# A scan's layernorm: its shift taken from VectorE's written order to GpSimd, behind the power

## The chip, the core and the metric

The kernel runs on one core of a Trainium2 chip. The metric is device time in microseconds (us), the median of several executions. The core has five engines that each work through a queue of their own: TensorE (PE, with its weight loads shown as PEld), VectorE (DVE), ScalarE (ACT), GpSimd (POOL) and SyncE (SP), which here only issues DMA transfers.

## The reference

There are 32 sequences of 256 tokens and 256 channels. A scan block comes first, two layers of windowed attention with a gated feed-forward part follow, and the input is added at the end. Cut to what matters:

```python
def scan_block(x, t_emb, ...):
    xr, gate = split(x @ W_in.T, 2)                  # 512 channels each
    xc = silu(conv4(xr + t_emb[:, None, :]))         # along the tokens
    mu, var = xc.mean(-1), xc.var(-1)
    xn = (xc - mu) / sqrt(var + 1e-5) * ln_g + ln_b  # the norm of this case
    Bm, Cm, dt = split(xn @ W_xproj.T, 3)            # 16 states each
    Ad = 1 + 0.01 * tanh(dt @ W_dt.T + b_dt) * A
    Bd = Bm * minimum(norm(xn), 1)
    # for every token: h = clip(h*Ad + Bd*xn, -10, 10); y = Cm . h
    return (y + D * xn) * silu(gate) @ W_out.T

def layer(x):                                        # twice
    q, k, v = split(shift_token(x) @ wqkv, 3)        # 8 heads of 64
    q, k = rotary(l2norm(q) * qs, l2norm(k) * ks)
    x = x + local_attention(q, k, v) @ wo            # window 128
    a, g = split(layernorm(shift_token(x)) @ w1 + b1, 2)
    return x + (a * gelu(g)) @ w2 + b2

out = x + layer(layer(scan_block(x, cond)))
```

## The kernel before

**Tiling.** The sequences form 4 groups of 8. A group's scan runs over 256 tokens in 8 chunks of 32 steps, so there are 32 chunks and 1024 steps in all. A step (`step`, L716) is one VectorE instruction of a custom form that updates the state h of 8 sequences by 16 states (128 partitions) over 512 channels. Its input comes from a scratch tensor `xnd` in DRAM, which holds the normed tokens of the chunk: `load_rows` (a DMA, `xrep<-xnd`) spreads one token's rows over the states, and ScalarE scales the tile (L706). TensorE reads the outcome out (`y`, L728).

**The norm of the scan.** A chunk has 256 token rows (8 sequences by 32 tokens), normed as two tiles of 128 rows, j = 0 and 1, which makes 64 norms. Each is a chain over four engines and a store:

1. `norm_turn`: TensorE transposes xc into `tp_x` (L548).
2. `norm_stats`: VectorE takes mean and variance into `mv` (bn_stats L558, bn_aggr L560) and adds the epsilon (`ve`, L562); GpSimd raises this to the power -1/2 (L565) into the first column of `stat`, the scale.
3. `norm_shift`: VectorE multiplies -mean by that scale (L571) into the second column of `stat`, the shift.
4. `norm_apply`: ScalarE computes xn = scale * tp_x + shift (L579).
5. `norm_affine`: GpSimd multiplies by ln_g and adds ln_b (L586, L587).
6. `norm_out`: SP stores xn to `xnd` (L591), and ScalarE sums the squares (L593).

**Attention and feed-forward.** While a group's scan runs, the sequences of the group before pass through the two layers, two sequence-layers for each chunk; so the first group's scan (`alone`) runs by itself, and after the last scan step only layers remain. Names that come up later: `ps_qkv` (L989) is the projection; `rotated` squares q or k (`sq`, L1002, ScalarE), forms `rot` and `swp` (L1005, L1010, VectorE) and finishes them on GpSimd (L1013, power `rn` L1021, L1022); `sc` and `pT` are scores and their exponentials (L1205, L1214; GpSimd masks them at L1225); `rs`, `ov` sum and multiply with the values (L1239, L1258); `divide` (L1282, VectorE) multiplies the heads' outputs `oT` by `rb`, the inverses of the sums; `ps_wo` (L1039) is the output projection; `pa` (L1362) is the feed-forward's first product, `ag` its GELU on ScalarE (L1373, with a load of the function's table) and then the gated product on VectorE (L1380); `po_f` (L1389) is the second product. In the second layer `fo` is that outcome (L1400, VectorE), GpSimd adds the input to it (L1408) and SP stores it (L1409). `sq`, `swp` and `fo` rotate through one set of three buffers, with the tag "swp". Of the scan, `xd` loads the normed rows for the skip term (L745), which GpSimd scales (L758), and `ps_in` (L399), the convolution's `acc` (L478, L489), `tz`, `zT` (L785, L799) and `ps_out` (L808) are its input and output parts.

**What sets the order.** The work of the scan is entered in slots, one for each step, by `at(s, what, ...)`; that of the layers in stages, by `stage(...)`. With s0 a chunk's first step, the norm j of that chunk has s = s0 - 26 + 4j; statistics stand in slot s+2, the shift in s+4, the application in s+5, the affine passes in s+6 and the store in s+9. The program is recorded in this order, and a list scheduler then chooses each engine's order by what it expects to be ready. `tc.keep_in_program_order(...)` takes an instruction out of this choice: it is held behind the instruction that was recorded before it on its engine. The shift L571 is held so, which puts it behind the scan step of slot s+4 on VectorE, and so are the scalings L706, the masks, `divide` and a few others. Every engine then works through its instructions in the order thus fixed.

Of the kernel before, what the change touches and what calls it, by code (L numbers as in the profile page):

```python
# [14 lines left out]
ALU = mybir.AluOpType  # L15
# [58 lines left out]
def kernel(  # L74
# [29 lines left out]
    nc = tc.nc  # L104
# [117 lines left out]
    def program(ctx, exact):  # L222
# [154 lines left out]
        def group_scan(g):  # L377
# [12 lines left out]
            ck = [{} for _ in range(NCH)]  # L390

            def at(s, what, *args):
                agendas[-1].setdefault(s, []).append(partial(what, *args))
# [161 lines left out]
            def norm_stats(c, j):  # L555
                tp, stat = ck[c]["tp", j], ck[c]["stat"]
                st = sm.tile([P, 6], FP, tag="st", name="st")
                nc.vector.bn_stats(st, tp)  # L558
                mv = sm.tile([P, 2], FP, tag="mv", name="mv")
                nc.vector.bn_aggr(mv, st)  # L560
                ve = sm.tile([P, 1], FP, tag="ve", name="ve")
                nc.vector.tensor_scalar_add(  # L562
                    ve, mv[:, 1:2], LN_EPS if alone else 4 * LN_EPS
                )
                nc.gpsimd.tensor_tensor(stat[:, j, 0:1], ve, neg_half[:, 0:1], ALU.pow)  # L565
                ck[c]["mv", j] = mv

            def norm_shift(c, j):
                stat, mv = ck[c]["stat"], ck[c].pop(("mv", j))
                tc.keep_in_program_order(  # L570
                    nc.vector.scalar_tensor_tensor(  # L571
                        stat[:, j, 1:2], mv[:, 0:1], -1.0, stat[:, j, 0:1], ALU.mult, ALU.mult
                    )
                )

            def norm_apply(c, j):
# [279 lines left out]
            for c in range(NCH):  # L856
                s0 = c * CH
                for hb in range(CH // TB):
                    s = s0 + hb * TB
                    for i in range(NI):  # L860
                        at(s + 4 * i + 5, read_out, c, hb, i)
                    at(s + 21, gated, c, hb)
                    at(s + 25, out_gate, c, hb)
                    at(s + 11, skip, c, hb)
                for ch in range(NC_):
                    at(s0 - 38 + 2 * ch, conv_in, c, ch)
                    at(s0 - 37 + 2 * ch, conv_taps, c, ch)
                    at(s0 - 36 + 2 * ch, conv_th, c, ch)
                    if not alone:
                        at(s0 - 35 + 2 * ch, conv_out, c, ch)  # L870
                for ch, s in enumerate((13, 16, 17, 18)):
                    at(s0 + s + 2, gate_th, c, ch)
                    if not alone:
                        at(s0 + s + 4, gate_out, c, ch)
                at(s0 - 25, raw_copy, c)
                at(s0 - 24, raw_turn, c)
                for j in range(NJ):
                    s = s0 - 26 + 4 * j
                    at(s + 2, norm_stats, c, j)
                    at(s + 4, norm_shift, c, j)  # L880
                    at(s + 5, norm_apply, c, j)
                    at(s + 6, norm_affine, c, j)
                    at(s + 9, norm_out, c, j)
                at(s0 - 11, length, c)
                at(s0 - 9, figures, c)
                at(s0 - 7, figures_in, c)
                at(s0 - 6, decay_th, c)
                at(s0 - 5, decays, c)
                at(s0 - 4, put_c, c, 0)
                at(s0 + 4, put_c, c, 1)  # L890
                for d in range(KM):
                    at(s0 + 45 + 2 * d, copy_y, c, d)
                    at(s0 + 46 + 2 * d, put_y, c, d)
            agendas.append({})
            for c in range(NCH):
# [20 lines left out]
                for hb in range(CH // TB):  # L916
                    s = s0 + hb * TB
# [5 lines left out]
            if alone:  # L923
                n = (NG - 1) * NCH * 2
                for u in range(n):
                    s = -30 + u * (NCH * CH) // n
# [6 lines left out]
        def scan_slots(groups):  # L933


            slots, scans = {}, [group_scan(g) for g in groups]
            for part in range(2):
                for i, agendas in enumerate(scans):
                    for s, what in agendas[part].items():
                        slots.setdefault(i * S + s, []).extend(what)  # L940
            for s in range(min(slots), max(slots) + 1):
                for what in slots.get(s, ()):
                    what()
                yield s
# [705 lines left out]
```

## Time and profile before

| | |
|---|---|
| median of 3 runs | 3600.9 us (3593.78 to 3604.1) |
| profiled execution | 3604.19 us, its span 3602.5 us |
| mean granted TensorE clock | 0.989 |
| TensorE from 0 to 310, 310 to 600 us | 274.7 of 310, 257.7 of 290 us busy |
| TensorE from 600 to 2810, 2810 to 3602 us | 2146.2 of 2210, 784.6 of 792 us busy |
| VectorE from 600 to 2810 us | 1781.0 of 2210 us busy |
| power L565 | 64 times, 541 to 1124 ns, median 562 |
| shift L571 | 64 times, 145 to 1264 ns, median 153 |
| application L579 | 64 times, 745 to 778 ns, median 777 |

The profile is of one execution, so times taken from it are set against its 3604.19 us. The span runs from the first to the last instruction, and 1.7 us of the execution lie around it. In a view of a line the three durations are the least, the median and the largest in ns; below them stands how long the engine sat idle before the line's instructions, with the releaser, the total and the number of times; and who waited for them. In a timeline a line gives start and duration in us, engine, line, operation, and "out<-in" with partitions by elements; the bracket tells idle time before it and what ended it. In the chain a line is start, length and what ran. "x8" means eight instructions in a row merged.

### The profile page before, as it was taken

The page shows a single profiled execution, that of the slowest core. Times are in us where ns is not written, and L with a number is a line of the kernel's source. Part 1 is how long each engine was busy: PE and PEld are TensorE (multiplying, and loading weights), DVE is VectorE, ACT ScalarE, POOL GpSimd, SP SyncE. Part 2 cuts the span into 40 slices and gives each one's busy share as a digit, 9 for nine tenths or more (in the row PEclk, how much of TensorE's full clock was granted, in tenths as well). Part 3 has the DMA queues.
Part 4 walks back from the last instruction along what each step waited for, and adds up shares of the span by engine and source line. Part 5 has one row for each costly group of instructions (what it writes and reads, how often), then busy time and mean ns, then how long its engine had stood idle before and what let it go on. Part 6 is the DMA issues. An engine that isn't in the chain of part 4 may idle for free.

```text
span 3602.5 us, 57609 instructions
## 1 busy us (share of the span) xinstructions
PE 3463.1 (96%) x20220; PEld 2254.4 (63%) x20220; DVE 2667.7 (74%) x5049; ACT 2148.9 (60%) x3659; POOL 1884.7 (52%) x1842
## 2 busy tenths in 40 slices
PE   7999988999999999999999999999999999999999
PEld 4545335666666666666666666666666677777777
DVE  5888889878888777887787888877877545555553
ACT  4656656666666666666666666666666544444543
POOL 4433466545556555655565556555544444443451
PEclk9999999999999999999999999999999999999999
DMA  7788755444454545444454555544454212011111
GB/s 201 210 217 219 200 154 148 133 110 138 131 140 130 149 140 146 130 114 126 117 140 128 135 149 137 142 106 130 116 141 123 61 38 61 13 30 39 31 27 37
DMA packets 468766, 435.67 MB, mean 121 GB/s; under 512 B 228723, under 2 KB 308084, under 8 KB 468340
## 3 DMA queue, kind: packets, MB, share of 16 engines
q1 hardware_dynamic: 384018, 419.88, 42.4%
q10 hardware_dynamic: 84450, 12.01, 2.0%
q8 instruction: 163, 2.67, 0.3%
q14 instruction: 135, 1.11, 0.1%
HBM read 383.54 MB, written 46.66 MB: 119 GB/s over the span
## 4 chain that ended last, share of the span: by engine, by line
PE 59%; DVE 19%; POOL 7%; DMA 7%; ACT 5%; issue 3%; SPq 0%; ACTq 0%; DVEq 0%; POOLq 0%
PE ps_qkv L989 12%; PE pa L1362 12%; DVE h L716 7%; PE po_f L1389 7%; DMA xrep<-xnd 5%; PE ps_wo L1039 4%; PE y L728 4%; PE ov L1258 3%; PE sc L1205 3%; DVE acc L489 3%; PE ps_out L808 2%; ACT xrep L706 2%; PE tr_qk L1028 2%; PE ps_in L399 2%; POOL rn L1021 2%
## 5 line engine op out<-in xcount | busy, mean ns | idle before, releaser
L716 DVE CUSTOM_DVE_ANT_0 h<-h,xrep,lim 128x512 f32<-128x512 f32 x1024 | 959.2, 937 | 219.2 <-ACT xrep L706 185.1
L706 ACT ACTIVATE xrep<-xrep,beta 128x512 f32<-128x512 f32 x960 | 674.2, 719 | 366.6 <-DMA xrep<-xnd 281.3
L989 PE MATMUL ps_qkv<-qkv,res 128*128 128x512 f32 x1536 | 718.5, 603 | 25.2 <-DVE ag L1380 9.8
L1362 PE MATMUL pa<-hT,w 128*128 128x256 f32 (+1 forms) x2816 | 679.9, 383 | 0.0
L1362 PEld LDWEIGHTS pa<-hT,w 128*128 128x128 f32 (+1 forms) x2816 | 516.2, 189 | 147.0 <-issue 53.8
L1013 POOL TENSOR_TENSOR rot<-rot,swp 128x512 f32<-128x512 f32 x256 | 340.1, 1328 | 442.7 <-DVE swp L1010 297.8
L989 PEld LDWEIGHTS ps_qkv<-qkv,res 128*128 128x128 f32 x1536 | 281.2, 191 | 314.1 <-issue 239.4
L1021 POOL TENSOR_TENSOR rn<-ss,neg_half 128x8 f32<-128x8 f32 x256 | 459.0, 1793 | 17.0 <-DVE ss L1019 6.9
L728 PE MATMUL y<-h,ly 128*32 128x512 f32 x2048 | 347.0, 611 | 18.9 <-DVE h L716 17.5
L1314 POOL TENSOR_TENSOR rstd<-ve,neg_half 128x2 f32<-128x2 f32 x64 | 47.0, 734 | 605.1 <-DVE ve L1312 587.7
L1389 PE MATMUL po_f<-ag,w 128*128 128x256 f32 x1280 | 309.7, 389 | 5.5 <-DVE fo L1400 4.3
L1022 POOL TENSOR_TENSOR rot<-rot,rn 128x512 f32<-128x512 f32 x256 | 289.3, 1130 | 19.9
L1380 DVE SCALAR_TENSOR_TENSOR ag<-pa,b_sb,ag 128x256 f32<-128x256 f32 x320 | 152.2, 476 | 195.8 <-ACT ag L1373 195.8
L1389 PEld LDWEIGHTS po_f<-ag,w 128*128 128x128 f32 x1280 | 237.3, 192 | 70.8 <-DVE xc L509 11.7
L1002 ACT ACTIVATE sq<-ps_qkv 128x512 f32<-128x512 f32 x256 | 151.9, 595 | 208.1 <-PE ps_qkv L989 145.5
L1373 ACT ACTIVATE ag<-pa,b_sb 128x256 f32<-128x256 f32 x320 | 150.1, 469 | 179.5 <-PE pa L1362 177.4
L489 DVE SCALAR_TENSOR_TENSOR acc<-xr,wc_sb,acc 128x256 f32<-128x256 f32 x384 | 197.7, 543 | 68.2 <-POOL acc L478 67.6
L1039 PE MATMUL ps_wo<-oT,wo 128*128 128x256 f32 x1024 | 231.6, 379 | 0.0
L1005 DVE TENSOR_TENSOR rot<-ps_qkv,rc_sb 128x512 f32<-128x512 f32 x256 | 174.5, 681 | 68.1 <-ACT sq L1002 67.9
L1214 ACT ACTIVATE pT<-sc 128x512 f32<-128x512 f32 x384 | 208.4, 596 | 6.8 <-PE sc L1205 4.8
L1039 PEld LDWEIGHTS ps_wo<-oT,wo 128*128 128x128 f32 x1024 | 194.6, 190 | 27.1 <-PE y L728 0.8
L1205 PEld LDWEIGHTS sc<-qT,kT 64*64 64x64 f32 (+1 forms) x2816 | 134.8, 159 | 114.6 <-issue 89.2
(159 smaller groups left out, 5689.8 us busy)
## 6 DMA issues: line engine op xcount, KB each, us to landing
xrep<-xnd SPq DMA_DIRECT2D x960, 256.0 KB
rb<-inv SPq DMA_DIRECT2D x128, 256.0 KB
xnd<-xn SPq DMA_DIRECT2D x64, 256.0 KB
qkv<-in_wqkv_dram SPq DMA_DIRECT2D x24, 512.0 KB
ahead<-xs_a SPq DMA_DIRECT2D x48, 256.0 KB
xp<-ahead SPq DMA_DIRECT2D x48, 256.0 KB
xd<-xnd SPq DMA_DIRECT2D x192, 64.0 KB
w<-in_w_dram SPq DMA_DIRECT2D x80, 128.0 KB
```

Of the source, the lines that this page charges most:

```text
L489: nc.vector.scalar_tensor_tensor(acc, xr[:, :, k : k + CH], wc_sb[:, ch, k : k + 1], acc, ALU.mult, ALU.add,)
L706: scaled = nc.scalar.activation(bx, ck[c].pop(("bx", t), bx), AF.Copy, scale=ck[c]["beta"][:, t : t + 1])
L716: nc.vector._custom_dve(TENSOR_ADD_SAT, out=h_new, in0=state["h"], in1=bx, s0=ck[c]["lim"][:, 0, t : t + 1], s1=ck[c]["lim"][:, 1, t : t + 1],
L728: nc.tensor.matmul(ck[c]["y", hb][32 * q : 32 * q + 32, :], ly[hb % 2][:, 32 * t : 32 * t + 32], ck[c].pop(("h", hb * TB + t)), start=(i = ...
L989: nc.tensor.matmul(ps, res[b][:, k, t0 : t0 + W], wt["qkv", a][:, k], start=(k == 0), stop=(k == KM - 1),)
L1013: nc.gpsimd.tensor_add(rot, rot, swp)
L1021: nc.gpsimd.tensor_tensor(rn, ss, neg_half, ALU.pow)
L1022: nc.gpsimd.tensor_mul(rot, rot, bc(rn, 2, DH))
L1039: nc.tensor.matmul(po[:, d], wt["wo", 0][:, c, d * P : (d + 1) * P], oT[:, c, :], start=(c == 0), stop=(c == NC_ - 1),)
L1205: nc.tensor.matmul(banks[r][k0 : k0 + mk, i, q0:q1], kT[rows, i0 + i, kw * W + k0 : kw * W + k0 + mk], qT[rows, i0 + i, kw * W + q0 : kw * ...
L1362: nc.tensor.matmul(dst[x], wt["w1", m][:, k, x], self.h[:, k], start=(k == 0), stop=(k == KM - 1),)
L1389: nc.tensor.matmul(self.po[:, d], wt["w2", 0][:, m, d * P : (d + 1) * P], self.ag[m], start=(m == 0), stop=(m == len(MCH) - 1),)
```

## The change

The shift is computed by GpSimd, as a tensor_scalar with two multiplications (mean times scale times -1), recorded directly behind the power. The slot entry for it, its function and its hold in VectorE's order are gone, and the mean no longer has to be handed on through `ck`.

```diff
@@ norm_stats
                 nc.gpsimd.tensor_tensor(stat[:, j, 0:1], ve, neg_half[:, 0:1], ALU.pow)
-                ck[c]["mv", j] = mv
-
-            def norm_shift(c, j):
-                stat, mv = ck[c]["stat"], ck[c].pop(("mv", j))
-                tc.keep_in_program_order(
-                    nc.vector.scalar_tensor_tensor(
-                        stat[:, j, 1:2], mv[:, 0:1], -1.0, stat[:, j, 0:1], ALU.mult, ALU.mult
-                    )
+                nc.gpsimd.tensor_scalar(
+                    stat[:, j, 1:2], mv[:, 0:1], stat[:, j, 0:1], -1.0, ALU.mult, ALU.mult
                 )
@@ the slots of a chunk
                 for j in range(NJ):
                     s = s0 - 26 + 4 * j
                     at(s + 2, norm_stats, c, j)
-                    at(s + 4, norm_shift, c, j)
                     at(s + 5, norm_apply, c, j)
                     at(s + 6, norm_affine, c, j)
                     at(s + 9, norm_out, c, j)
```

## The prediction

> **What bounds the kernel now.** The page first. Its first part lists each engine's busy time, its fourth the chain of work that ended last, by engine:
>
> ```profile
> PE 3463.1 (96%) x20220; PEld 2254.4 (63%) x20220; DVE 2667.7 (74%) x5049; ACT 2148.9 (60%) x3659; POOL 1884.7 (52%) x1842
> ...
> PE 59%; DVE 19%; POOL 7%; DMA 7%; ACT 5%; issue 3%; SPq 0%; ACTq 0%; DVEq 0%; POOLq 0%
> ```
>
> TensorE is 96% busy, yet holds only 59% of the chain, so stages differ. From 2810 us on there is no scan, and nothing of the change. While scan and attention run side by side a chunk lasts about 103 us (one sequence's ps_wo stands at 1624.13, the next chunk's at 1726.55, the next at 1829.61). One such chunk in the chain, start and length:
>
> ```profile
> 1716.40 3.43 PE ps_qkv L989 x8
> ...
> 1732.60 1.73 PE pa L1362 x8
> ...
> 1748.79 1.73 PE ps_qkv L989 x4
> 1750.54 0.60 ACT sq L1002
> 1751.17 0.69 DVE rot L1005
> ```
>
> From 1700 to 1750 every link is TensorE, back to back; from 1750 to 1801 the chain runs through ACT, DVE, POOL and the xrep transfer, and starts from TensorE's last product. So in the first half a delay elsewhere is free while it is shorter than TensorE's slack, and what exceeds it shifts the second half one to one. The changed instruction stands in the first half. Its own line view:
>
> ```profile
> L571 DVE SCALAR_TENSOR_TENSOR stat<-mv,stat x64: 145/153/1264, 30.2 to 2657.8; 128x1 f32<-128x1 f32 x64
> ...
>   POOL stat L565: 41.9, 22
> ...
>   ACT xn L579: 105.9, 38
> ```
>
> DVE sat idle 41.9 us for POOL's power in 22 of 64 cases, and ACT 105.9 us for the shift in 38. These are the apparent prize. Neither is on the chain above.
>
> **What the skill says.** (1) "SBUF — State Buffer", section "Who interferes with whom": DVE and GpSimd have one port pair that is locked for a whole instruction; a DVE instruction with two SBUF inputs holds off a GpSimd one that reads SBUF. The trace agrees: the power L565 takes 541 ns at best and 1124 at most, fo L1408 1259 to 2226. (2) "TensorE: Matmul & The Clock Gate", "Architectural detail": ACT, DVE and GpSimd take their queues strictly in order. The timelines below agree: ACT stands still with later work ready.
>
> **The change, part by part.** *Removed:* 64 DVE instructions of 153 ns (18.9 us busy, many overlapped with a neighbour) and the 41.9 us of waits. *Added:* 64 POOL instructions. The trace has no such form on one column; the nearest row is lim L660, a tensor_scalar on 32 columns:
>
> ```profile
> L660 POOL TENSOR_SCALAR lim<-pi x32: 291/296/617, 45.1 to 2708.0; 128x32 f32<-128x32 f32 x32
> ```
>
> I take 0.29 us; at most 0.62 as there, at least 0.1 (POOL's 128x2 memset takes 0.09). 64 x 0.29 = 19 us on an engine that is 52% busy. By itself I cost it at nothing, under POOL's idle time; without that cover it is 0.3 us per norm, the 19 us. The hop from POOL back to DVE goes; POOL follows itself after 0.08 us, as L587 does L586.
>
> *Moved,* as the order that the scheduler gives each engine in the two kernels shows (settled when a kernel is built; there is no time in it). On DVE and TensorE nothing else moves from chunk 10 on. On POOL the shift, and xn's two affine passes L586/L587, come directly behind the power, ahead of fo L1408 where that stood between. On SP the store of xn follows them ahead of fo's store L1409. On ACT, for the first norm (j=0) of chunks 18 to 31, **xn L579 moves ahead of the GELU's table load, ag L1373 and sq L1002**, with two xrep scalings behind it. Before, ACT did those during the power; in the new order it waits. ACT, layer 0, before:
>
> ```profile
> 1714.77 1.28 ACT L1373 ACT_TABLE_LOAD   x1
> 1716.43 0.47 ACT L1373 ACTIVATE ag<-pa,b_sb 128x256 f32<-128x256 f32 x1 [0.38 <-PE pa L1362]
> 1718.15 0.60 ACT L1002 ACTIVATE sq<-ps_qkv 128x512 f32<-128x512 f32 x1 [1.24 <-PE ps_qkv L989]
> 1718.64 0.77 ACT L579 ACTIVATE xn<-tp_x,stat 128x512 f32<-128x512 f32 x1
> ```
>
> DVE and POOL there:
>
> ```profile
> 1717.15 1.22 DVE L1282 TENSOR_TENSOR oT<-oT,rb 128x1024 f32<-128x1024 f32 x1
> 1718.29 0.15 DVE L571 SCALAR_TENSOR_TENSOR stat<-mv,stat 128x1 f32<-128x1 f32 x1
> 1718.36 0.48 DVE L1380 SCALAR_TENSOR_TENSOR ag<-pa,b_sb,ag 128x256 f32<-128x256 f32 x1
> ```
>
> ```profile
> 1716.20 1.05 POOL L565 TENSOR_TENSOR stat<-ve,neg_half 128x1 f32<-128x1 f32 x1 [0.90 <-DVE ve L562]
> ```
>
> *Layer 0 (8 chunks: 20 to 23, 28 to 31).* The power ends at 1717.25, just after L1282 (two SBUF inputs) has begun; the POOL shift is held off to 1718.37 and ends at 1718.65, 0.2 later than DVE's. ACT, free at 1714.75, waits 3.9 us; then xn to 1719.4, two xreps to 1720.65, table load to 1721.95, ag to 1722.44: 5.5 us later than before (1716.90). The product L1380 starts at 1722.5, +4.1. All DVE work behind it (rot, swp, ss) is 3.8 to 4.2 late, and hence POOL's rn and rot, the power of j=1 (queued behind them) and its xn, +2.8. TensorE's slack, time from each input's end to the matmul that takes it: tp_x after L1380 5.3, pa after the first swp 4.5, ps_wo after the second 3.6 against 3.8 late, **ov after the second xn 1.74 against 2.8**. So +1.1 us a chunk (0.2 to 2). DVE's vanished wait for j=1 (2.67 us) is spent on this lateness.
>
> *Layer 1, which writes the output (6 chunks: 18, 19, 24 to 27).* POOL and ACT before:
>
> ```profile
> 2233.60 1.04 POOL L565 TENSOR_TENSOR stat<-ve,neg_half 128x1 f32<-128x1 f32 x1 [0.91 <-DVE ve L562]
> 2234.71 2.18 POOL L1408 TENSOR_TENSOR fo<-fo,xs 128x512 f32<-128x512 f32 x1
> ```
>
> ```profile
> 2236.94 0.78 ACT L579 ACTIVATE xn<-tp_x,stat 128x512 f32<-128x512 f32 x1 [0.74 <-DVE stat L571]
> ...
> 2240.42 0.60 ACT L1002 ACTIVATE sq<-ps_qkv 128x512 f32<-128x512 f32 x1 [2.09 <-POOL xn L587]
> ```
>
> The releaser named is doubtful: sq and fo share a rotating buffer ("swp", three deep), and the second sq may only start when fo is stored, 3.5 us after fo's end at 2236.89. The view of fo's tile has the same:
>
> ```profile
>   ACT sq L1002: 39.3, 24
> ```
>
> In the new order the shift ends at about 2236.05 (0.9 earlier than now), xn runs to 2236.8, its affine passes to 2239.6, and only then fo to 2240.9: 4.0 later. Its store lands at 2244.4, and the second sq and swp are 4.0 late. ps_wo has 1.31 us of slack there: **+2.7 us a chunk** (0 to 3.7: nothing if the store isn't what frees the buffer). SP's queue stops at fo's store 4 us longer; behind it stand weight loads, xd's four loads (issued from 2238.80, wanted by POOL's L758 only at 2249.10, so 0 while they are less than about 5 us late) and xrep loads, which are not issued before 2246.47 as it is: 0. The other TensorE inputs late there (3.0 to 3.6 of slack against about the same lateness, ov 0.8) fit within those 2.7.
>
> *Chunks 8 to 17:* many places differ, xn mostly earlier and fo later. I take -2 (-10 to +10), a choice. *First 600 us, scan alone:* the shift stood 2.3 and 4.7 us behind its power in DVE's order without a stall; 20 of them cost DVE 0.15 us each, and xn comes up to 3 us sooner, but is not on the chain (xrep transfer 17.4%, scan step 16.9% of it). I take -3 (-6 to 0). *After 2810 us:* 0.
>
> Sum: 6 x 2.7 + 8 x 1.1 - 2 - 3 = 16.2 + 8.8 - 5 = +20. The profiled execution took 3604.2 us (span 3602.5, 1.7 around it), 3.3 above the median of the three runs, 3600.9 (3593.8 to 3604.1). Against itself the sum is 3624; against the median, which I forecast, **3621**. About 0.3%, 11 us, is what a measurement of this kernel can tell from no change.
>
> **Rivals.**
> (a) *Faster:* the j=1 stall is the real limiter. TensorE waits for DVE's ag, h and ag again (sc 19.4, y 17.5, ps_qkv 9.8, ov 7.5: 54 us in its list of waits). If half of DVE's 41.9 us is behind those, and ACT's new wait hides, the result is 3601 - 21 = 3580, with a third 3587. For it: POOL's power for j=1 and its DVE wait hold the scan steps behind them. Against: DVE then meets a 2.83 us wait for xrep at 1736.58, so that the time is only passed on. It decides if ACT's ag comes less than about 1.3 us late, not 5.5.
> (b) *Nothing:* slacks are wider than read (the releaser at 2240.42 is right after all, and xn j=1 makes good its delay): +0 to +9, about 3603.
> (c) *Much slower:* the shift is held off by a scan step or L1282 in every chunk, ACT stops each time, and chunks 8 to 17 lose as the later ones do: 24 x 2 = 48, 3649.
> That the shift is not moved at all is excluded: the order has it behind each power.
>
> **How the numbers follow.** The likeliest case (+11 to +33) gets 0.45, (c) 0.10, (b) 0.20, (a) 0.25. Slower by over 0.3%: 0.55; within: 0.20; faster: 0.25. Own range of the likeliest: 3612 to 3634. The range to hold 8 in 10 leaves out the far ends of (a) and (c): 3581 to 3646.
>
> **What would show it.** Right: in the profile after, no L571 on DVE; POOL's shift about 0.3 us, over 1 us where L1282 runs; ACT's idle time before xn grows above the 111.7 us it has before from all causes, ag's product late; fo's store later and ps_wo of layer 1 about 2.7 late within its chunk; TensorE busy time unchanged, chunks 24 to 27 longest in growth. Wrong: chunks of 103 us or less in 2200 to 2600 us, or xn without a wait on ACT; then (b) or (a).

## The result, and the profile after

The changed kernel takes 3634.1 us in the median of six runs (3630.5 to 3641.3), against 3600.9 us before (3593.8 to 3608.7). The ratio is **1.0095, with a 95% interval of 1.0082 to 1.0108**: 33 us slower. The profiled execution has a span of 3636.1 us, and its scan ends 33.9 us later than before's; what follows the last scan step takes the same 791 us in both.

First the parts of the page that were shown of before, busy times and the chain by engine:

```profile
PE 3474.4 (96%) x20220; PEld 2258.5 (62%) x20220; DVE 2653.5 (73%) x4985; ACT 2147.0 (59%) x3659; POOL 1912.4 (53%) x1906
...
PE 51%; DVE 18%; POOL 13%; DMA 7%; ACT 6%; issue 4%; SPq 0%; ACTq 0%; DVEq 0%; POOLq 0%
```

No engine has got appreciably more work: DVE lost 14 us, POOL gained 28. But TensorE's share of the chain has gone from 59 to 51%, and POOL's from 7 to 13%. The chain now leaves TensorE in a part of the chunk where it used not to.

In the changed file the lines from the norm's application on stand 6 or 7 lower: the shift is L566 (POOL), xn L573, ag L1366 (ACT) and L1373 (DVE), `divide` L1275, sq L995, ps_wo L1032, ov L1251, fo's addition L1401. The line view of the new shift:

```profile
L566 POOL TENSOR_SCALAR stat<-mv,stat x64: 259/444/1146, 32.3 to 2693.3; 128x1 f32<-128x1 f32 x64
...
  ACT xn L573: 182.3, 50
```

DVE's 41.9 us of waits for the power are gone from its list. **ACT's wait for the shift has grown from 105.9 us (38 times) to 182.3 us (50 times).** A chunk with layer 0, the same place as before, first ACT:

```profile
1734.60 0.72 ACT L700 ACTIVATE xrep<-xrep,beta 128x512 f32<-128x512 f32 x1 [1.53 <-issue]
1739.09 0.78 ACT L573 ACTIVATE xn<-tp_x,stat 128x512 f32<-128x512 f32 x1 [3.76 <-POOL stat L566]
1739.76 1.32 ACT L700 ACTIVATE xrep<-xrep,beta 128x512 f32<-128x512 f32 x2
1741.10 1.28 ACT L1366 ACT_TABLE_LOAD   x1
1742.40 0.47 ACT L1366 ACTIVATE ag<-pa,b_sb 128x256 f32<-128x256 f32 x1
```

DVE and then POOL in the same stretch:

```profile
1737.71 1.21 DVE L1275 TENSOR_TENSOR oT<-oT,rb 128x1024 f32<-128x1024 f32 x1
1742.90 0.48 DVE L1373 SCALAR_TENSOR_TENSOR ag<-pa,b_sb,ag 128x256 f32<-128x256 f32 x1 [3.98 <-ACT ag L1366]
```

```profile
1736.76 1.04 POOL L565 TENSOR_TENSOR stat<-ve,neg_half 128x1 f32<-128x1 f32 x1 [0.91 <-DVE ve L562]
1737.91 1.14 POOL L566 TENSOR_SCALAR stat<-mv,stat 128x1 f32<-128x1 f32 x1
```

ACT stands 3.76 us ahead of xn, while the table load and ag, which need nothing of the norm, stand behind it. DVE has to wait 3.98 us for ag. The shift ends with `divide`, which had begun before it. How this reaches TensorE is told by the chain of that chunk:

```profile
1737.91 1.15 POOL stat L566
1739.09 0.78 ACT xn L573
1739.86 1.22 ACT xrep L700 x2
1741.10 1.28 ACT L1366
1742.40 0.48 ACT ag L1366
1742.90 0.48 DVE ag L1373
...
1752.93 1.72 POOL xd L752
1754.64 0.96 POOL stat L565
1756.00 0.79 ACT xn L573
1756.83 2.82 PE ov L1251 x32
```

From xn of the first norm (j=0) the delay goes by ag and DVE's product to q's and k's rotation on POOL, by the queue there to the power of the second norm, and by its xn to TensorE's ov. In before's chunk the same twenty microseconds of the chain were all TensorE.

The table says where the 33.9 us arise. It takes, at each chunk's last scan step, the time since the span's start, and how much the two traces' difference has grown within those chunks. Chunks are counted here by the steps that run. The norms of chunk c are formed during the steps of chunk c-1; so what the prediction calls chunks 18, 19, 24 to 27, by the norm, are 17, 18, 23 to 26 here.

| chunks, by their steps | growth, us | predicted |
|---|---|---|
| 0 to 16, of which | 13.0 | -5 (two terms, -3 and -2) |
| ... 0 to 7 | 4.8 | |
| ... 8 to 12, 14 to 16 | 0.7 | |
| ... 13 | 7.4 | |
| 17, 18, 23 to 26 (layer with output) | 16.6 | 6 x 2.7 = 16.2 |
| 19 to 22, 27 to 30 (other layer) | 4.2 | 8 x 1.1 = 8.8 |
| 31 | 0.0 | 0 |

One rival that the prediction doesn't name is TensorE's clock, whose mean grant is 0.985 here against 0.989 in before's profile. The trace has it at half for 110.5 us in all, in pieces of 3.4 to 10.2 us, and before's for 82.7 us; by estimate from these two, that costs at most half of the difference, 14 us. It isn't the cause of the loss: e4 below, with the changed order on ScalarE and TensorE, has 82.5 us at half clock and is still 30.2 us longer than before in its trace. From chunk 17 to 31 the two have 13.7 and 10.2 us at half clock, at most 1.8 of the 20.9 us lost there.

### The profile page after: what moved, and what is told of

Same layout as the page of the kernel before. It is cut to its first block, busy times and chain, and to the rows that moved or that the text cites. A ratio compares the mean times of both kernels' runs of the same rounds, so it can differ in the third digit from the quotient of the medians.

```text
span 3636.1 us, 57714 instructions
## 1 busy us (share of the span) xinstructions
PE 3474.4 (96%) x20220; PEld 2258.5 (62%) x20220; DVE 2653.5 (73%) x4985; ACT 2147.0 (59%) x3659; POOL 1912.4 (53%) x1906
## 3 DMA queue, kind: packets, MB, share of 16 engines
q8 instruction: 163, 2.67, 0.3%
## 4 chain that ended last, share of the span: by engine, by line
PE 51%; DVE 18%; POOL 13%; DMA 7%; ACT 6%; issue 4%; SPq 0%; ACTq 0%; DVEq 0%; POOLq 0%
PE ps_qkv L982 11%; PE pa L1355 10%; DVE h L710 7%; PE po_f L1382 6%; DMA xrep<-xnd 5%; PE y L722 3%; PE ov L1251 3%; POOL rn L1014 3%; PE ps_wo L1032 3%; PE sc L1198 3%; DVE acc L489 3%; ACT xrep L700 3%; PE ps_out L802 2%; PE ps_in L399 2%; PE tr_qk L1021 2%
## 5 line engine op out<-in xcount | busy, mean ns | idle before, releaser
L710 DVE CUSTOM_DVE_ANT_0 h<-h,xrep,lim 128x512 f32<-128x512 f32 x1024 | 956.7, 934 | 234.1 <-ACT xrep L700 198.4
L1373 DVE SCALAR_TENSOR_TENSOR ag<-pa,b_sb,ag 128x256 f32<-128x256 f32 x320 | 152.5, 477 | 260.1 <-ACT ag L1366 260.1
L995 ACT ACTIVATE sq<-ps_qkv 128x512 f32<-128x512 f32 x256 | 150.7, 595 | 206.1 <-PE ps_qkv L982 129.9
L1366 ACT ACTIVATE ag<-pa,b_sb 128x256 f32<-128x256 f32 x320 | 150.2, 470 | 165.1 <-PE pa L1355 162.8
L1032 PE MATMUL ps_wo<-oT,wo 128*128 128x256 f32 x1024 | 234.4, 383 | 10.6 <-DVE swp L1003 6.9
L1032 PEld LDWEIGHTS ps_wo<-oT,wo 128*128 128x128 f32 x1024 | 194.8, 191 | 42.1 <-issue 15.5
```

Of the source, the lines that this page charges most:

```text
L710: nc.vector._custom_dve(TENSOR_ADD_SAT, out=h_new, in0=state["h"], in1=bx, s0=ck[c]["lim"][:, 0, t : t + 1], s1=ck[c]["lim"][:, 1, t : t + 1],
L1032: nc.tensor.matmul(po[:, d], wt["wo", 0][:, c, d * P : (d + 1) * P], oT[:, c, :], start=(c == 0), stop=(c == NC_ - 1),)
```

## The experiments

The kernel before was run beside each, with medians of 3604.3 to 3604.9 us there; times are medians, ratios those to before. Each run's file has its own line numbers, so L716, L714, L712 or L710 can be the same scan step.

**e1, the hold alone.** The shift stays on DVE and in its slot, only the hold is taken away:

```diff
-                tc.keep_in_program_order(
-                    nc.vector.scalar_tensor_tensor(
-                        stat[:, j, 1:2], mv[:, 0:1], -1.0, stat[:, j, 0:1], ALU.mult, ALU.mult
-                    )
+                nc.vector.scalar_tensor_tensor(
+                    stat[:, j, 1:2], mv[:, 0:1], -1.0, stat[:, j, 0:1], ALU.mult, ALU.mult
                 )
```

> The kernel before with one thing changed: the shift stays on VectorE in slot s+4, but without the hold. Its place in ScalarE's order then equals the changed kernel's (xn ahead of table load, ag and sq), with no added GpSimd instruction. Theory A (the time is lost because ScalarE, once the hold is gone, gets xn ahead of ag and stands still for the power): 3620 to 3645, most of the +33. Theory B (the 64 GpSimd instructions and their port lock cost it): 3601, no difference that can be told.

Measured: 3702.6 us, ratio 1.0271 (1.0254 to 1.0287), **three times the loss of the change**. Neither theory had that. DVE now stops for the power, early in its order. DVE in e1 at the second norm of a chunk, then TensorE:

```profile
1764.57 0.15 DVE L562 TENSOR_SCALAR ve<-mv 128x1 f32<-128x1 f32 x1
1769.00 0.16 DVE L570 SCALAR_TENSOR_TENSOR stat<-mv,stat 128x1 f32<-128x1 f32 x1 [4.29 <-POOL stat L565]
1769.08 4.45 DVE L714 CUSTOM_DVE_ANT_0 h<-h,xrep,lim 128x512 f32<-128x512 f32 x3
1773.46 0.47 DVE L1378 SCALAR_TENSOR_TENSOR ag<-pa,b_sb,ag 128x256 f32<-128x256 f32 x1
```

```profile
1773.99 1.51 PE L1237 MATMUL rs<-pT,head_cols 128*32 128x256 f32 x32 [3.29 <-DVE ag L1378]
```

The product ag stands behind the shift and three scan steps, and TensorE waits 3.29 us for it (56 us in 14 such waits by its list of waits). Its clock also stood at half for 68 us in chunks 17 to 31, against 10 in before, which by estimate is up to 29 of the 84 us that it lost there. So losing the hold is bad wherever the shift is computed, and with the hold gone GpSimd is the better place for it. As e1 adds DVE's stop, it doesn't size the change's loss; e2 does.

**e2, the hold put back on an empty instruction.** The shift stays on GpSimd. DVE clears one column of xn's tile in slot s+4, held, and xn is written over it:

```diff
+            def norm_mark(c, j):
+                xn = sp.tile([P, DI], FP, tag="xn", name="xn", bufs=2)
+                tc.keep_in_program_order(nc.vector.memset(xn[:, 0:1], 0.0))
+                ck[c]["xn", j] = xn
...
-                xn = sp.tile([P, DI], FP, tag="xn", name="xn", bufs=2)
+                xn = ck[c]["xn", j]
...
+                    at(s + 4, norm_mark, c, j)
                     at(s + 5, norm_apply, c, j)
```

> The changed kernel, shift on GpSimd behind the power, with the hold put back on an empty instruction: VectorE clears one column of xn's tile in slot s+4, held, and xn follows it. ScalarE's order is then exactly that of the kernel before; VectorE no longer waits for the power. Theory A: 3590 to 3606, at least all of the +33 comes back. Theory B: 3630, as the changed kernel. Rival C (VectorE's 41.9 us of waits were worth something by themselves): 3570 to 3590.

Measured: 3604.5 us, ratio **0.9997** (0.9987 to 1.0007). The whole loss is gone with the shift still on GpSimd. In its trace not only ScalarE but all five engines take their instructions in the order of before (four DMA issues on ScalarE in the first 130 us apart). So e2 shows that the new orders cost the time; which engine's order does, it can't tell. Here the traces help: in the chunks of the other layer from 19 on, ScalarE's is the only engine's order that the change alters (and with it the place of xn's store on SP); in those of the layer with output, GpSimd's is altered too, fo behind the affine passes.

And the wait that the change removes from DVE is worth nothing: here it is removed too (DVE's list has no wait for the power), with no gain. DVE at the second norm shows where it went, before and then in e2:

```profile
1732.99 0.16 DVE L571 SCALAR_TENSOR_TENSOR stat<-mv,stat 128x1 f32<-128x1 f32 x1 [2.67 <-POOL stat L565]
...
1736.58 0.81 DVE L716 CUSTOM_DVE_ANT_0 h<-h,xrep,lim 128x512 f32<-128x512 f32 x1 [2.83 <-ACT xrep L706]
```

```profile
1735.22 0.81 DVE L714 CUSTOM_DVE_ANT_0 h<-h,xrep,lim 128x512 f32<-128x512 f32 x1 [5.81 <-ACT xrep L704]
```

DVE's wait for the power (2.67 us) has become 2.98 us more of waiting for xrep. Over the whole span its waits for xrep are 185.1 us before and 231.2 us in e2: 46 us more, where 41.9 us of waits for the power are gone.

**e3, GpSimd's load alone.** The kernel before, with the same instruction computed once more on GpSimd behind each power, into a spare column:

```diff
+                ext = sm.tile([P, 1], FP, tag="ext", name="ext", bufs=2)
+                nc.gpsimd.tensor_scalar(
+                    ext, mv[:, 0:1], stat[:, j, 0:1], -1.0, ALU.mult, ALU.mult
+                )
                 ck[c]["mv", j] = mv
```

> The kernel before with a spare GpSimd instruction behind each power: it computes the same shift into a column that nobody reads; VectorE's held shift stays. Price of 64 GpSimd instructions of 0.3 to 1.1 us in GpSimd's queue alone. Theory A: 3598 to 3606. Theory B: 3625 to 3640.

Measured: 3604.3 us, ratio 1.0002 (0.9994 to 1.0011). The added instructions, held off by DVE or not, cost nothing where nobody waits for them.

**e6 and e7, which norms and which chunks.** e2 with the empty instruction for j=0 only, and from chunk 18 on (by the norm) only:

```diff
-                    at(s + 4, norm_mark, c, j)
+                    if j == 0:                     # e6
+                        at(s + 4, norm_mark, c, j)
...
+                    if g * NCH + c >= 18:          # e7
+                        at(s + 4, norm_mark, c, j)
```

> As e2, but the empty held instruction for the first norm of a chunk (j=0) only; the second is left as in the changed kernel. If the loss comes from xn of j=0 going ahead of ag on ScalarE: chunks 18 to 31 lose nothing, and the time is 3600 to 3610. If the second norm's place counts as well: 3610 to 3625.

> As e2, but the empty held instruction from chunk 18 on only. If the profile's reading by chunks holds (16 us lost by the end of chunk 17, 18 after it): 3601 + 16 = 3617, and no further loss from chunk 18 on. If the loss of the late chunks depends on a lead or lag brought over from the early ones: not additive, below 3608 or above 3625.

e6: 3607.8 us, ratio 1.0009 (0.9998 to 1.0020). Losing the hold of the first norm makes nearly all of the loss; from chunk 17 to the scan's end e6 grows by 0.4 us. But e6 doesn't leave the second norm as in the changed kernel, as was expected: in its trace every engine's order from 1240 us on is that of before, the second xn's place on ScalarE included. Which hold decides is shown; what the second norm's place would cost alone is not. (Its profile is 7.8 us late, but 8.6 us of this arise in the first chunk, where the clock stood at half from 23.7 to 51.0 us.)

e7: 3618.5 us, ratio 1.0041 (1.0022 to 1.0060), 14 us over before. Its growth by the end of chunk 16 is 15.3 us, and after it none. So the losses of the two halves are separate and add up. Up to there its clock stood at half for 75 us, against 68 in before, so by estimate at most 3.4 of the 15.3 us are the clock's.

**e11, one place in the early half.** Chunk 13 is the largest lasting item (chunk 8 grows by 8.0 us, but chunk 9 makes 7.4 of it good). ACT and TensorE of the changed kernel there:

```profile
935.25 0.78 ACT L573 ACTIVATE xn<-tp_x,stat 128x512 f32<-128x512 f32 x1 [9.76 <-POOL stat L566]
```

```profile
936.08 3.78 PE L802 MATMUL ps_out<-zT,w_out_sb 128*128 128x256 f32 x8 [4.45 <-ACT xn L573]
```

The xn of j=1 has gone ahead of two hT and two pT, and its power is queued on POOL behind rn, rot and xd. Before, it stood behind them, and ACT waited 5.35 us, while TensorE ran on without a stop:

```profile
922.98 1.99 PE L808 MATMUL ps_out<-zT,w_out_sb 128*128 128x256 f32 x8
```

Eight such products took 1.99 us there and 3.78 in the changed kernel: its clock stood at half from 934.9 to 941.7 us. All four traces with this wait of 4.4 us (the changed kernel's, e4's, e7's and e9's) have such a stretch here, 3.4 or 6.8 us long; the nine without the wait have none at this place. So this wait cost more than its length. That it brought on the half clock is likely from this, but no run tests it.

The empty instruction was put back for chunk 14's norms alone (`if g * NCH + c == 14`).

> The changed kernel with the empty held instruction of e2 at the two norms of chunk 14 only, where xn of j=1 stands ahead of hT and waits 9.8 us for the power in the changed kernel. By the profile this one place costs 7 us (chunk 13 is 108.5 long against 101.1): the growth within chunk 13 falls below 2 us, and the time is 3634 - 7 = 3627. If the loss only moves: chunk 13 as long as in the changed kernel.

In the trace chunk 13 grows by 0.5 us in place of 7.4, and TensorE's wait of 4.45 us is not in its list any more. The time, 3637.1 us, ratio 1.0090 (1.0057 to 1.0123), can't tell 7 us from none. The early chunks of this execution were some 4 us later than those of the changed kernel's profile by chunk 12; from there to the end it grows by 19.0 us against 25.3. The place is shown; its size rests on one trace. Since e11 marks both norms, it doesn't say which one's; in e6, where only the first is marked, the second xn stands behind hT and pT again, and chunk 13 grows by 0.5 us too.

**e8, no wait of ACT at all.** The changed kernel with xn held in ACT's own order two slots earlier:

```diff
-                nc.scalar.activation(
-                    xn, tp, AF.Identity, bias=stat[:, j, 1:2], scale=stat[:, j, 0:1]
+                tc.keep_in_program_order(
+                    nc.scalar.activation(
+                        xn, tp, AF.Identity, bias=stat[:, j, 1:2], scale=stat[:, j, 0:1]
+                    )
                 )
...
-                    at(s + 5, norm_apply, c, j)
+                    at(s + 3, norm_apply, c, j)
```

> The changed kernel with xn held in ScalarE's order at slot s+3, which puts it behind ag, both sq and pT, where the power is long done, for j=0, and behind yo for j=1. ScalarE's waits for the power, 182 us in the changed kernel and 106 before, should all but vanish. If these waits cost time even in the kernel before: faster than it, 3575 to 3597. If TensorE hides them there: 3597 to 3606.

Measured: 3627.6 us, ratio 1.0063 (1.0048 to 1.0078); both expectations missed. From the norms of chunk 18 on, the wait ahead of xn is zero, where before has 75 us. Yet from chunk 17 to the end this kernel is no faster than before but grows by 3.0 us: **removing those 75 us gained nothing, as they stood beside a busy TensorE**. The other 16.4 us arise by the end of chunk 16, where this order is another one and still waits 46.7 us; which of its places costs them wasn't pursued.

**e4, e9, e10 and e5, the store of fo.** In the layer with output the prediction blames the late addition and store of fo. The changed kernel there, POOL, ACT and TensorE:

```profile
2268.70 1.28 POOL L1401 TENSOR_TENSOR fo<-fo,xs 128x512 f32<-128x512 f32 x1
```

```profile
2272.62 0.60 ACT L995 ACTIVATE sq<-ps_qkv 128x512 f32<-128x512 f32 x1 [3.08 <-DMA out_dram<-fo]
```

```profile
2274.77 3.69 PE L1032 MATMUL ps_wo<-oT,wo 128*128 128x256 f32 x16 [1.50 <-issue]
...
2284.76 2.82 PE L1251 MATMUL ov<-pT,v_sb 128*64 128x256 f32 x32 [0.53 <-ACT xn L573]
```

In all, TensorE's waits ahead of ps_wo in the six chunks are 1.50 to 2.25 us long, 10.6 us together; before has none there.

e4 forms fo in the residual's tile, so that sq doesn't wait for the store:

```diff
-                    self.fo[:, d] if last else rv,
+                    rv,
...
-                    nc.gpsimd.tensor_add(self.fo, self.fo, xs)
-                    nc.sync.dma_start(out=outT[:, :, b, :], in_=self.fo)
+                    fo = res[self.b][:, :, 1:]
+                    nc.gpsimd.tensor_add(fo, fo, xs)
+                    nc.sync.dma_start(out=outT[:, :, b, :], in_=fo)
```

> The changed kernel with the last layer's output formed in the residual's own tile, so that sq no longer waits for the store of fo. Theory A's second half (in the second layer the late fo and its store hold sq, swp and ps_wo): 1.5 us less in each of chunks 18 and 24 to 26 and some in the chunks before 18, 3618 to 3630. If the store is not what holds sq: 3634.

Measured: 3641.3 us, ratio 1.0096 (1.0083 to 1.0110), no gain. The wait had only moved; POOL in e4 now stops for the same store, ahead of the memset for the next residual, and the rotation is behind it:

```profile
2269.70 0.10 POOL L948 MEMSET res<- 128x2 f32 x1 [2.66 <-DMA out_dram<-res]
```

e9 forms the outcome in the residual's tile as e4 does, but sums it into the input's tile, out of another set of buffers, and stores from there; e10 does so on the kernel before. The part that differs from e4:

```diff
-                    nc.gpsimd.tensor_add(self.fo, self.fo, xs)
-                    nc.sync.dma_start(out=outT[:, :, b, :], in_=self.fo)
+                    nc.gpsimd.tensor_add(xs, res[self.b][:, :, 1:], xs)
+                    nc.sync.dma_start(out=outT[:, :, b, :], in_=xs)
```

> The changed kernel; the last layer's output is summed into the tile of the input (xs, another set of four buffers) and stored from there, so that neither sq nor the next residual waits for the store. If the late store is what costs the second layer: TensorE's 1.5 us wait ahead of ps_wo is gone, chunks 24 to 26 grow by at most 1 us each against before, and the time is 5 to 9 us under the changed kernel's. If GpSimd's order costs it in another way (rot is late there too): chunks 24 to 26 still grow by 2 us or more.

> The same edit on the kernel before, as the other half of the comparison: there sq waits 39 us for the store in all, but ps_wo has 1.3 us of slack. 3598 to 3606, no change; if the wait costs even there, 3585 to 3597.

e9: 3632.9 us, ratio 1.0083 (1.0057 to 1.0109), inconclusive as a time. In its trace the six chunks grow by 11.3 us in place of 16.6, less than was expected. The store still holds something, now a rot, which rotates through the same buffers as the input's tile, and TensorE still waits. DVE and TensorE of e9:

```profile
2266.95 0.69 DVE L998 TENSOR_TENSOR rot<-ps_qkv,rc_sb 128x512 f32<-128x512 f32 x1 [1.05 <-DMA out_dram<-xs]
```

```profile
2268.47 3.69 PE L1032 MATMUL ps_wo<-oT,wo 128*128 128x256 f32 x16 [0.83 <-ACT xrep L700]
```

e10: 3604.6 us, ratio 0.9996 (0.9988 to 1.0005). Before, the store is early enough and its buffer costs nothing.

e5 leaves the buffers as they are and puts fo's addition back ahead of xn's affine passes, by holding these in POOL's order:

```diff
-                nc.gpsimd.tensor_mul(xn, xn, lng_sb)
+                tc.keep_in_program_order(nc.gpsimd.tensor_mul(xn, xn, lng_sb))
```

> The changed kernel with xn's first affine pass held in GpSimd's order, which puts both passes behind the rotation's work and fo's addition back ahead of them; ScalarE keeps xn ahead of ag. If the late store of fo is what costs the second layer its time: TensorE's 1.5 us wait ahead of ps_wo is gone in chunks 24 to 26, these chunks lose at most 1 us each instead of 2.4, and in all 5 to 9 us less than the changed kernel (3625 to 3629 at a before of 3601). If it is xn's place on ScalarE alone: no difference from the changed kernel.

Measured: 3704.5 us, ratio 1.0274 (1.0256 to 1.0292), far off both expectations, in part for a reason that neither named: the passes now stand right ahead of the second norm's power, its xn is later still, and TensorE waits for it in all 14 chunks from 17 to 30, 41.4 us together. These chunks grow by 63.6 us; the clock stood at half for 34 us in them, against 10 in before. The other 38 us, up to chunk 16, weren't followed. TensorE of e5 in the layer with output, all that it waits for from 2308 to 2360 us:

```profile
2334.49 4.50 PE L1251 MATMUL ov<-pT,v_sb 128*64 128x256 f32 x32 [3.00 <-ACT xn L573]
```

The wait ahead of ps_wo is gone in all six chunks, though ACT waits for xn (3.78 us) just as in the changed kernel. With fo early there is no wait at ps_wo; with its store's buffer moved on, the wait shrinks from 1.50 to 0.83 us as the store's hold shrinks. So fo's lateness and its store are what holds ps_wo, as far as these traces show it; both kernels differ in other ways too, and a clean kernel without the store's hold wasn't tried.

None of these kernels beats the kernel before beyond the intervals; e2, e3 and e10 equal it, and e6 can't be told from it.

## Why the prediction was right

The direction and the mechanism were right: 33 us slower against 20, within the range, at the very end of the likeliest case's own (to 3634). The sum was right in its largest term, twice too large in another and wrong in sign in the rest. Point by point:

- **The prize was worth nothing.** Right. DVE's removed wait reappears as a wait for xrep (e2), and ACT's 75 us of waits in the late chunks are hidden (e8). Neither was on the chain. Rival (a) falls with these two.
- **The new order, ACT's above all, is what costs.** Right: with every engine's order back the loss is zero (e2), and the first norm's hold decides nearly all of it (e6). In the chunks of the other layer only ACT's order has changed; in those with output GpSimd's shares in it, as was predicted. The wait of 3.9 us is 3.76 in the trace.
- **The layer with output, 6 x 2.7.** 16.6 us measured against 16.2, in part by luck. In the chunk shown TensorE waits 1.50 us at ps_wo and 0.53 at ov, where the prediction had 2.7 at ps_wo covering ov; the six waits at ps_wo are 10.6 us, not 16.2. sq's wait for the store was read rightly although the view of before named another releaser. The chunk grew by 2.2; the other 0.2 us is not in these two waits.
- **The other layer, 8 x 1.1.** Mis-sized: 0.53 each. The ov of the second norm is the place, as predicted, but TensorE waits 0.34 us in the chunk shown. ov's slack of 1.74 was exceeded by that, so xn was 2.1 us late instead of 2.8. One part of it is seen on POOL: the second power rn took 1.65 us, against 2.08 before, when DVE was in its way.
- **Chunks 8 to 17 and the first 600 us, -2 and -3.** This is the step that failed: together +13.0 instead of -5. An earlier xn was counted as harmless or a gain. In chunk 13 the prediction's own mechanism was at work, on the second norm, which the prediction didn't look at there: xn ahead of hT, a wait of 9.76 us, 7 us lost (e11), of them 4.45 as TensorE's wait and a part in the half clock beside it. In the first 450 us the loss is no chance of one trace. From the end of chunk 0, whose length differs by up to 10 us between traces, to that of chunk 7, the eight kernels without the hold there lose 2.7 to 12.0 us, those with it (e2, e3, e10) -1.6 to +1.1. e6, with the first norm's hold alone, loses 4.7 in its one trace, so there the second norm's seems to count as well. The cause of this part wasn't isolated.
- **POOL's load.** Right that 64 instructions cost nothing by themselves (e3). Their price was too low: 259 ns at the least, but 575 in the mean (36.8 us busy, not 19), since 34 of the 64 took over 350 ns, 16 of them beside `divide` and the others beside a scan step; the one shown took 1.14 us beside `divide`, as foretold. The trace agrees with the Trainium skill, "SBUF — State Buffer", section "Who interferes with whom".
- **Rival (c),** the port lock in every chunk, falls with e2 and e3: the lock is there, and it costs no time while ACT does other work. Rival (b) falls with the result.

## What to carry to other kernels

In this program an instruction held in one engine's order also set when its result was expected, and so the order of other engines: with the hold gone, its consumers moved forward, to stand there and block what is behind them (e1, and the change itself), and an empty held instruction put them back (e2). Before moving a small instruction, compare the whole orders of its consumers' engines, and price what now stands behind a wait by the slack of the engine that bounds the stage. And a wait that is long but lies in a stage which another engine fills is no prize: look for it in the chain first. If the wait does reach TensorE, look at the granted clock beside it: here it stood at half around a wait of 4.45 us.

## What was not expected of the hardware

A 128x1 tensor_scalar took 259 ns on POOL at the least, 444 in the median and 1146 at the most in the changed kernel; in e2, the same instruction with other neighbours, the median was 272. A DVE memset of one column took 59 ns.
